# The projection's seventh product by quarter products, with GpSimd adding its parts

## Chip, cores and metric

The kernel runs on one core of one Trainium2 chip. The metric is the device time of one execution in microseconds (us). The kernel before takes 3261.11 us, the median of 3 runs (3260.39 to 3261.24).

TensorE is called PE in the profile and here, its weight loads PEld, VectorE DVE, ScalarE ACT, GpSimd POOL, and SP is the engine that issues the transfers.

## The reference

The reference applies two layers of the same form to x of shape (8, 512, 32, 32), all in fp32. One layer, cut to what matters (the layers differ in the number of groups and in their weights):

```python
xn = group_norm(x) * gn_scale + gn_bias            # (B, 512, N), N = 32 * 32
q, k, v = split(einsum('oc,bcn->bon', qkv_w, xn) + qkv_b)   # 8 heads of 64
attn = softmax(einsum('bhdi,bhdj->bhij', q, k) / sqrt(64))
out = einsum('bhij,bhdj->bhdi', attn, v)
return einsum('oc,bcn->bon', proj_w, out) + proj_b + x
```

The last line is the projection with which this change deals: a 512x512 weight matrix times a 512x1024 matrix for each of 8 batches in 2 layers.

## The kernel before, in words

The kernel goes through 16 units, one for each layer and batch. Each unit u does its three input projections (`projections`: q, k, v), then the output projection of the unit before it (`project(old, after)`), then its own attention (`attention`). The projection of unit 15 stands at the end and has a function of its own (`project_last`). So `project` runs 15 times, in units 1 to 15.

**Seven products in place of eight.** `blocks` computes a matrix product in a Strassen-Winograd form. Both matrices are cut into 2x2 blocks, sums and differences of blocks are made beforehand (`left[k]` and `right[k]`, k from 1 to 7), and seven products of blocks, 256x256 by 256x512, are added up. In `blocks` they come in the order 1, 6, 2, 7, 5, 4, 3, with the banks of PSUM called bx (`apair[0]`), by (`sbank[0]`) and bz (`apair[1]`): 1 and 2 write bx, 6, 7 and 4 write by, 5 and 3 write bz. Product 7 accumulates onto product 6 in by. Engines DVE and ACT take intermediate results out: p1 is product 1, u2 is p1 plus product 6, u3 is p1 plus products 6 and 7. Then the blocks of the result are c11, and by `others` u3 + product 5 for (1, 1), p1 + product 4 on by for (1, 0), and u2 + product 5 + product 3 for (0, 1).

**Quarter products.** A product k named in `INNER` is cut once more in the same way: seven matmuls of 128x256 in place of four matmuls of 128x512 (`inner_products`, with the matmul on line L458; an uncut product runs in `block_product`, L419). Its seven steps write as follows. Steps 2, 3 and 4 accumulate into the product's own bank. Steps 1, 6 and 7 accumulate one after the other onto a quarter of a helper bank `one`, and ACT copies the running sum out after each of them (L463). Step 5 writes a helper bank `two` and is copied too. So a step 6 or 7 can start only when ACT has copied what stood in `one` before it. The four copies land in a room in SBUF (`rest`, in the profile m_o for the projection). `fold` (L471, L472) has GpSimd add them up in place, and `rests` (L748) has GpSimd add the room into the finished result, after which it is stored. The order of the steps is one of three tuples:

```python
ORDER, ORDER_5, ORDER_1 = (1, 2, 3, 6, 5, 4, 7), (1, 5, 2, 6, 3, 4, 7), (2, 3, 1, 4, 5, 6, 7)
```

ORDER_1 is used for product 1 of k. There, and for no other product, the last step is not run in its place: `inner_products` returns it, and the next uncut product runs it between its own matmuls.

**The projection.** `project` calls `blocks` with products 2, 3 and 4 cut (tiles ro, their right factors, and lo, their left factors); product 7 is uncut. After each product `done` runs: DVE adds bias and residual to u2, u3 and p1 (`plus`, L706), and DVE takes the statistics of the next unit's input (L283). `others` takes banks on DVE (L740). Attention's first scores wait for the takes of (1, 0), the third scores for those of (0, 1).

**Right and left factors.** The right factors of the projection come from the attention output ao. The list `parts` in `attention` puts the subtractions on DVE (`mix_right` L179, `mix_inner_in` L209 to L212, `mix_o` L1019) behind numbered steps of the next unit's `projections`: steps 15 to 21 lie in v. The left factors of the cut products are the same for all units of a layer. GpSimd makes them once per layer (`mix_inner_left`, L226 to L232, four additions for each product), and they are stored in memory and loaded in each unit (tiles lo and a spare quarter of ro). Layer 0's are made in unit 0, layer 1's for the projection in unit 9. In unit 7, GpSimd also makes three sets of left factors of layer 1's q (tile lw), inside `project`, after its third `done`.

**Order of work.** The schedule is manual: each engine runs its instructions in the order in which the code issues them. The framework adds the semaphores that data and buffers need.

Of the kernel before, what the change touches and what calls it, by code (L numbers as in the profile page):

```python
# [11 lines left out]
F32 = mybir.dt.float32  # L12
# [20 lines left out]
def fast_path(ctx, tc, x, qkv_wT, proj_wT, vecs, groups, out, flag):  # L33
# [24 lines left out]
    BL = 32  # L58
    SCALE = 1.0 / math.sqrt(D)

    INNER = {"q": (2, 5, 4, 3), "k": (1, 2, 7, 5, 4, 3), "o": (2, 3, 4)}
    assert D == H and C == FD

    def pool(name, bufs, **kw):
# [358 lines left out]
                )  # L423

    def blocks(name, left, right, tokens, c11, others, done, u3_in, summed, inner={}, rests=None,
               u2_in=(trpool, "tr"), between=None, behind=None, p1=None):

        bx, by, bz = apair[0], sbank[0], apair[1]
        sums, taken = [], []

        def products(bank, k, start, stop, between=None):
            block_product(bank, left[k], right[k], tokens, start, stop, between)

        def inner_products(bank, k, first=False):  # L440

            if k not in inner:
                products(bank, k, first, k != 5)
                return None
            a, b, one, two, order, room = inner[k]
            one, two, rest = one[:, 0, :FD2], two[:, 0, :FD2], room(f"m{k}_{name}")
            dst = {
                1: one, 6: one, 7: one, 5: two,  # L450
                2: bank[:, 0, :FD2], 3: bank[:, 0, FD2:], 4: bank[:, 1, :FD2],
            }
            to = {
                1: rest[:, 0, :FD2], 6: rest[:, 0, FD2:], 7: rest[:, 1, :FD2], 5: rest[:, 1, FD2:]
            }

            def step(j):
                nc.tensor.matmul(  # L458
                    dst[j], a[j], b[j], start=j in (1, 5) or first and j in (2, 4),
                    stop=j not in (1, 6), skip_group_check=True,  # L460
                )
                if j in to:
                    taken.append(nc.scalar.copy(to[j], dst[j]))  # L463

            for j in order if k != 1 else order[:-1]:
                step(j)
            return (rest, partial(step, order[-1])) if k == 1 else rest

        def fold(rest):
            add = nc.gpsimd.tensor_add  # L470
            add(rest[:, 0, FD2:], rest[:, 0, FD2:], rest[:, 1, FD2:])  # L471
            add(rest[:, 1, FD2:], rest[:, 1, :FD2], rest[:, 1, FD2:])  # L472

        def add_rest(r, h, rest, alone=None):

            if rest is not None:
                fold(rest)
                rests(r, h, rest, alone)

        def work(pool, tag, k):  # L480
            sums.append(pool.tile([P, 2, FD], F32, tag=tag, name=f"{k}_{name}"))
            return sums[-1]

        fresh = p1 is not None or 1 in inner
        if p1 is not None:
            sums.append(p1)
            done(sums)
            products(by, 6, True, False)
        elif fresh:
            p1 = work(accpool, "acc", "p1")  # L490
            rest, last = inner_products(bx, 1, True)
            done(sums)
            products(by, 6, True, False, last)
            add = nc.vector.tensor_add
            add(rest[:, 0, FD2:], rest[:, 0, FD2:], rest[:, 1, FD2:])
            add(p1[:, 0, :], bx[:, 0, :], rest[:, 0, :])
            add(p1[:, 1, :FD2], bx[:, 1, :FD2], rest[:, 1, :FD2])
            add(p1[:, 1, FD2:], rest[:, 1, :FD2], rest[:, 1, FD2:])
        else:
            products(bx, 1, True, False, between)  # L500
            if behind is not None:
                behind()
            p1 = work(accpool, "acc", "p1")
            nc.scalar.copy(p1, bx)  # L504
            done(sums)
            products(by, 6, True, False)
        u2 = work(*u2_in, "u2")
        summed(0, u2, by, p1)
        done(sums)
        rest = inner_products(bx, 2, fresh)  # L510
        c11(bx, p1 if fresh else None, rest)
        add_rest(0, 0, rest)
        done(sums)
        seventh = inner_products(by, 7)
        u3 = work(*u3_in, "u3")
        summed(1, u3, by, p1)
        if seventh is not None:
            fold(seventh)
        done(sums)
        twice = inner_products(bz, 5, True)  # L520
        others(1, 1, bz, u3, twice)
        add_rest(1, 1, twice, u3)
        if seventh is not None:
            rests(1, 1, seventh)
        done(sums)
        rest = inner_products(by, 4)
        others(1, 0, by, p1)
        add_rest(1, 0, rest)
        if seventh is not None:
            rests(1, 0, seventh)  # L530
        done(sums)
        rest = inner_products(bz, 3)
        others(0, 1, bz, u2, twice)
        add_rest(0, 1, rest, u2 if twice is not None else None)
        if twice is not None:
            rests(0, 1, twice)
        done(sums)
        return taken[-1:]
# [159 lines left out]
    def project(w, after):  # L698


        l, b = units[w.u]
        dst = mid[b] if l == 0 else out[b]
        g = 0

        def plus(to, o, cols, more):
            return nc.vector.scalar_tensor_tensor(  # L706
                to, cols, vec[:, l, PB, o : o + 1], more, ALU.add, ALU.add
            )

        def done(sums):  # L710

            nonlocal g
            g += 1
            for i in range(2):
                if g == 2:
                    u2 = sums[1][:, i, :]
                    plus(u2, i, w.res[i][:, FD:], u2)
                elif g == 4:
                    u3 = sums[2][:, i, :]
                    plus(u3, 2 + i, w.res[2 + i][:, FD:], u3)  # L720
                elif g == 5:
                    p1 = sums[0][:, i, :]
                    plus(p1, 2 + i, w.res[2 + i][:, :FD], p1)
            after(g)

        results = {}

        def store(o, h):
            nc.sync.dma_start(dst[o * P : (o + 1) * P, ts(h, FD)], results[o, h])

        def c11(bank, *_):
            for i in range(2):
                cols = results[i, 0] = w.res[i][:, :FD]
                plus(cols, i, bank[:, i, :], cols)

        def others(r, h, bank, more, _=None):
            for i in range(2):
                o = 2 * r + i
                results[o, h] = more[:, i, :]
                w.evac[h] = nc.vector.tensor_add(more[:, i, :], bank[:, i, :], more[:, i, :])  # L740
                if (r, h) == (1, 1):
                    store(o, h)

        def rests(r, h, rest, _):
            for i in range(2):
                o = 2 * r + i
                cols = results[o, h]
                nc.gpsimd.tensor_add(cols, cols, rest[:, i, :])  # L748
                store(o, h)

        w.evac = [None, None]
        x, z, s1 = apair[0], apair[1], sbank[1]
        tmp = room_of(tmppool, "tmp")
        plan = {
            2: (s1, z, ORDER, tmp), 4: (x, s1, ORDER, tmp), 3: (s1, x, ORDER, room_of(accpool, "acc"))
        }
        inner = {k: (*w.inner_o[k], *plan[k]) for k in w.inner_o}
        w.taken = blocks(
            f"o_{w.u}", w.left, w.right_o, False, c11, others, done, (rbpool, "rb"), plain_sum, inner, rests
        )  # L760

    def project_last(w, rest):
# [25 lines left out]
    def attention(w, at_step, at_end):  # L788
# [188 lines left out]
        def bias_last():  # L977
# [4 lines left out]

        parts = {
            3: [lambda: reciprocals(CC - 1)], 10: [lambda: divide(CC - 1)], 14: [bias_last],
            17: mixing[:2], 21: [mixing[3], mixing[2]],
        }

        w.inner_o = {}
# [15 lines left out]
            w.making[i](lefts[3 * i : 3 * i + 3], later=behind_loads)  # L1004

        def mix_o(k):
            tag = {2: "x2", 3: "x1", 4: "x4"}[k]
            room = tpool.tile([P, 4, FD2], F32, tag=tag, name=f"ro{k}_{u}")
            if k == INNER["o"][-1]:
                w.inner_o[k] = mix_inner_in(w.right_o[k], room, nc.vector)  # L1010
                lefts.append(room[:, 3, :P])
                if u == B:
                    make_left(2)
                else:
                    nc.sync.dma_start(lefts[-1], src[:, len(lefts) - 1, :])
            else:
                w.inner_o[k], subs = mix_inner(w.right_o[k], room, nc.vector)
                for part in subs:
# [4 lines left out]
                w.inner_o[k] = (inner_lefts(k, w.left[k], lefts[3 * i : 3 * i + 3]), w.inner_o[k])  # L1023

        parts[15] = [load_left]
        if u == B:
            parts[20] = [partial(make_left, 0), partial(make_left, 1)]
        parts[18] = [partial(mix_o, 2)]
        parts[21] += [partial(mix_o, 4), partial(mix_o, 3)]
        w.finish = finish  # L1030
        return parts

# [451 lines left out]
```

## Time and profile before

| | us | share of the span |
|---|---|---|
| span of the profiled run | 3260.1 | |
| PE busy | 3247.2 | 100% |
| DVE busy | 2713.7 | 83% |
| ACT busy | 1650.7 | 51% |
| POOL busy | 1238.9 | 38% |

A row of the profile names the line of the kernel, the engine, the operation, what it writes and reads, and shapes. A row of a timeline begins with the start and the duration in us, merges equal instructions (x8 is eight of them), and ends in brackets with the idle time of the engine just before and what released it. Each matmul of the code is two records on PE[...]. The ends of matmuls are modelled, and overlap the next start; distances from start to start are what counts. A row of the waits reads: engine and line that waited, who released it, total us, times, longest us.

### The profile page before, as it was taken

What the parts mean: (1) busy time and instruction counts of PE and PEld (TensorE: products, weight loads), DVE (VectorE), ACT (ScalarE), POOL (GpSimd) and SP (SyncE); (2) the same over time, 40 slices, a digit from 0 to 9 for tenths busy, and PEclk for the clock granted to TensorE, in tenths of its full rate; (3) what the DMA queues carried; (4) which work ended last, traced back from release to release, by engine and by line L of the source; (5) the groups of instructions that cost most, each with busy time, mean ns of one, the idle gap of its engine ahead of it and who ended that gap; (6) DMA issues with size and microseconds to landing.
All of it is one profiled execution on the core that took longest, in us unless ns stands there. A gap on an engine that the chain in (4) does not pass through costs nothing.

```text
span 3260.1 us, 56861 instructions
## 1 busy us (share of the span) xinstructions
PE 3247.2 (100%) x22206; PEld 1858.1 (57%) x22206; DVE 2713.7 (83%) x3460; ACT 1650.7 (51%) x2296; POOL 1238.9 (38%) x1235
## 2 busy tenths in 40 slices
PE   9999999999999999999999999999999999999999
PEld 5456474654746547465474655747556474564743
DVE  5887978889788897889978889797897978979777
ACT  1653726536274463744637446374563735637354
POOL 2054071531706317065470632607226071350710
PEclk9999999999999999999999999999999999999999
DMA  3112120121201212023120121201212012120221
GB/s 102 43 52 79 44 78 28 49 79 46 79 28 45 79 46 87 20 71 107 58 89 29 45 80 52 85 15 45 86 46 85 15 49 82 46 85 15 70 74 48
DMA packets 86465, 192.53 MB, mean 59 GB/s; under 512 B 22960, under 2 KB 34992, under 8 KB 84272
## 3 DMA queue, kind: packets, MB, share of 16 engines
q1 hardware_dynamic: 86192, 188.82, 17.0%
q8 instruction: 180, 2.95, 0.4%
q14 instruction: 93, 0.76, 0.1%
HBM read 148.00 MB, written 39.19 MB: 57 GB/s over the span
## 4 chain that ended last, share of the span: by engine, by line
PE 97%; DVE 1%; issue 1%; ACT 0%; DMA 0%; SPq 0%; DVEq 0%; ACTq 0%
PE a L851 26%; PE s L823 25%; PE s L419 14%; PE a L419 12%; PE a L458 10%; PE s L458 9%; PE a L823 1%; DVE acc L870 1%; PE s L769 0%; PE a L769 0%; PE s L364 0%; DVE tr L883 0%; DMA xn<-x_dram 0%; DVE acc L868 0%; ACT p L831 0%
## 5 line engine op out<-in xcount | busy, mean ns | idle before, releaser
L831 ACT ACTIVATE p<-s 128x1024 f32<-128x1024 f32 x976 | 997.0, 1023 | 560.4 <-PE s L823 526.3
L851 PE MATMUL a<-p,v 64*64 64x512 f32 x8192 | 1098.2, 589 | 1.7 <-ACT p L831 1.5
L823 PE MATMUL s<-q,k 64*64 64x512 f32 x7808 | 1056.4, 590 | 0.0
L870 DVE TENSOR_TENSOR acc<-acc,p 128x1024 f32<-128x1024 f32 x768 | 964.0, 1255 | 71.1 <-ACT p L831 18.1
L851 PEld LDWEIGHTS a<-p,v 64*64 64x64 f32 x8192 | 381.0, 131 | 500.5 <-ACT p L831 352.8
L823 PEld LDWEIGHTS s<-q,k 64*64 64x64 f32 x7808 | 380.1, 133 | 435.3 <-issue 425.6
L1080 POOL TENSOR_TENSOR r<-xn 128x256 f32<-128x256 f32 x30 | 51.2, 1707 | 1126.3 <-DVE acc L870 1049.0
L653 POOL TENSOR_TENSOR k<-k,m_k 128x512 f32<-128x512 f32 x180 | 259.7, 1464 | 0.0
L868 DVE TENSOR_TENSOR acc<-p,p 128x1024 f32<-128x1024 f32 x128 | 157.6, 1231 | 23.0 <-ACT p L831 13.9
L883 DVE STREAM_TRANSPOSE tr<-acc 128x1024 f32<-128x1024 f32 x128 | 157.9, 1233 | 0.0
L315 POOL TENSOR_TENSOR y<-var,half 128x4 f32<-128x4 f32 (+1 forms) x17 | 33.1, 1949 | 327.2 <-DVE var L313 327.2
L653 POOL TENSOR_TENSOR q<-q,m_q 128x512 f32<-128x512 f32 x120 | 157.1, 1325 | 0.0
L893 DVE TENSOR_REDUCE red<-tr 128x32 f32<-128x1024 f32 x128 | 153.9, 1202 | 0.5
L541 DVE TENSOR_TENSOR u_v<-s,p_v 128x1024 f32<-128x1024 f32 x32 | 39.2, 1224 | 124.6 <-PE s L419 122.3
L877 DVE TENSOR_TENSOR ao<-a,tmp 128x512 f32<-128x512 f32 x128 | 87.9, 687 | 65.9 <-ACT tmp L876 65.9
L504 ACT COPY p_o<-a 128x1024 f32<-128x1024 f32 x15 | 15.2, 1012 | 244.2 <-PE a L419 244.2
L471 POOL TENSOR_TENSOR m_o<-m_o 128x256 f32<-128x256 f32 x45 | 34.0, 756 | 253.9 <-ACT m_o L463 253.9
L463 ACT COPY m_q<-s 128x256 f32<-128x256 f32 x150 | 55.8, 372 | 145.8 <-PE s L458 143.1
L419 PE MATMUL s<-x_t,s2w 128*128 128x512 f32 x256 | 117.5, 592 | 0.0
L419 PE MATMUL a<-w,xn 128*128 128x256 f32 x496 | 112.1, 379 | 0.0
L463 ACT COPY m_k<-s 128x256 f32<-128x256 f32 x165 | 61.4, 372 | 93.9 <-PE s L458 90.3
L337 ACT ACTIVATE xn<-xn,shift,scale 128x512 f32<-128x512 f32 x124 | 99.5, 804 | 12.4 <-DVE shift L333 12.2
(283 smaller groups left out, 5150.5 us busy)
## 6 DMA issues: line engine op xcount, KB each, us to landing
rb<-drec SPq DMA_DIRECT2D x128, 256.0 KB, 3.8
xn<-mid SPq DMA_DIRECT2D x36, 512.0 KB, 7.6
il<-ilk SPq DMA_DIRECT2D x15, 1152.0 KB, 6.6
xn<-x_dram SPq DMA_DIRECT2D x32, 512.0 KB, 7.2
x<-x_dram SPq DMA_DIRECT2D x32, 512.0 KB, 5.3
x<-mid SPq DMA_DIRECT2D x28, 512.0 KB, 4.8
il<-ilq SPq DMA_DIRECT2D x15, 768.0 KB, 4.2
mid<-u_o SPq DMA_DIRECT2D x32, 256.0 KB, 2.1
```

The source lines that it names most:

```text
L337: nc.scalar.activation(cols, cols, AF.Identity, bias=st["shift"][:, c - lo : c - lo + 1], scale=st["scale"][:, c - lo : c - lo + 1],)
L419: nc.tensor.matmul(dst, at[:, c, ts(i, P)], moving[:, c, :], start=start and c == 0 and not (tokens and i % 2), stop=stop and c == 1, skip ...
L458: nc.tensor.matmul(dst[j], a[j], b[j], start=j in (1, 5) or first and j in (2, 4), stop=j not in (1, 6), skip_group_check=True,)
L463: taken.append(nc.scalar.copy(to[j], dst[j]))
L653: w.last[sel].append(add(cols, cols, rest[:, i, :]))
L823: nc.tensor.matmul(bank[e * H : (e + 1) * H, j, :], w.k[pr][j * H : (j + 1) * H, t * P + e * H : t * P + (e + 1) * H], w.q[pr][j * H : (j ...
L831: exp = nc.scalar.activation(p, bank, AF.Exp, scale=SCALE)
L851: nc.tensor.matmul(banks[r][j * H : (j + 1) * H, :], w.v[rows, t, lo : lo + D], p[rows, j, :], start=(t == 0), stop=(t == NT - 1),)
L868: nc.vector.tensor_add(acc, state["first"], p)
L870: nc.vector.tensor_add(acc, acc, p)
L883: nc.vector.transpose(tr, state["acc"].pop(c))
L893: nc.vector.tensor_reduce(red[:, :, qh, :], state["tr"].rearrange("p j (f i) -> p j f i", i=BL), AX.X, ALU.add)
```

## The change

Product 7 of the projection is cut into quarter products too, so that its four matmuls of 512 columns become seven of 256. It uses the helper banks `one` = sbank[1] and `two` = apair[1], ORDER_1 as order of the steps, and the room o2.

Its parts have to be added into two results, (1, 1) and (1, 0). For (1, 0) GpSimd adds the folded room into p1 itself (`into_p1`), before DVE adds the bias to p1 and before the takes; for (1, 1) `rests` adds it after the take, and `rests` now also stores (1, 1). Product 3's room moves from the pool accpool to o1, as the right factors of product 7 get a tile from accpool. The subtraction `mixing[3]` moves one step ahead (20 in place of 21), because product 7's right factor comes from it.

```diff
-    INNER = {"q": (2, 5, 4, 3), "k": (1, 2, 7, 5, 4, 3), "o": (2, 3, 4)}
+    INNER = {"q": (2, 5, 4, 3), "k": (1, 2, 7, 5, 4, 3), "o": (2, 3, 7, 4)}
...
         if seventh is not None:
             fold(seventh)
+            if into_p1:
+                for i in range(2):
+                    nc.gpsimd.tensor_add(p1[:, i, :], p1[:, i, :], seventh[:, i, :])
         done(sums)
...
-        if seventh is not None:
+        if seventh is not None and not into_p1:
             rests(1, 0, seventh)
...
-                if (r, h) == (1, 1):
-                    store(o, h)
-
-        def rests(r, h, rest, _):
+
+        def rests(r, h, rest, _=None):
...
         plan = {
-            2: (s1, z, ORDER, tmp), 4: (x, s1, ORDER, tmp), 3: (s1, x, ORDER, room_of(accpool, "acc"))
+            2: (s1, z, ORDER, tmp), 7: (s1, z, ORDER_1, room_of(tpool, "o2")),
+            4: (x, s1, ORDER, tmp), 3: (s1, x, ORDER, room_of(tpool, "o1")),
         }
...
-            17: mixing[:2], 21: [mixing[3], mixing[2]],
+            17: mixing[:2], 20: [mixing[3]], 21: [mixing[2]],
...
-            tag = {2: "x2", 3: "x1", 4: "x4"}[k]
-            room = tpool.tile([P, 4, FD2], F32, tag=tag, name=f"ro{k}_{u}")
-            if k == INNER["o"][-1]:
+            pool, tag = {2: (tpool, "x2"), 7: (accpool, "acc"), 3: (tpool, "x1"), 4: (tpool, "x4")}[k]
+            room = pool.tile([P, 4, FD2], F32, tag=tag, name=f"ro{k}_{u}")
+            if k in (7, 4):
                 w.inner_o[k] = mix_inner_in(w.right_o[k], room, nc.vector)
-                lefts.append(room[:, 3, :P])
-                if u == B:
-                    make_left(2)
-                else:
-                    nc.sync.dma_start(lefts[-1], src[:, len(lefts) - 1, :])
+                n = len(lefts)
+                lefts.extend(room[:, 3, i * P : (i + 1) * P] for i in range(2))
+                if u != B:
+                    nc.sync.dma_start(
+                        room[:, 3, :].rearrange("p (s o) -> p s o", s=2), src[:, n : n + 2, :]
+                    )
...
         parts[15] = [load_left]
+        parts[18] = [partial(mix_o, 2)]
+        parts[20].append(partial(mix_o, 7))
+        parts[21] += [partial(mix_o, 4), partial(mix_o, 3)]
         if u == B:
-            parts[20] = [partial(make_left, 0), partial(make_left, 1)]
-        parts[18] = [partial(mix_o, 2)]
-        parts[21] += [partial(mix_o, 4), partial(mix_o, 3)]
+            parts[20] += [partial(make_left, i) for i in range(3)]
+            parts[21].append(partial(make_left, 3))
```

More of the change, by code (lines that the diff above doesn't have):

```diff
@@ L425, in blocks @@
     def blocks(name, left, right, tokens, c11, others, done, u3_in, summed, inner={}, rests=None,
-               u2_in=(trpool, "tr"), between=None, behind=None, p1=None):
+               u2_in=(trpool, "tr"), between=None, behind=None, p1=None, into_p1=False):
         bx, by, bz = apair[0], sbank[0], apair[1]
@@ L758, in project @@
         w.taken = blocks(
-            f"o_{w.u}", w.left, w.right_o, False, c11, others, done, (rbpool, "rb"), plain_sum, inner, rests
+            f"o_{w.u}", w.left, w.right_o, False, c11, others, done, (rbpool, "rb"), plain_sum, inner, rests,
+            into_p1=True,
         )
```

## The prediction

> **What bounds the kernel now.** I read the page's busy shares and chain first, to see which engine sets the end.
>
> ```profile
> PE 3247.2 (100%) x22206; PEld 1858.1 (57%) x22206; DVE 2713.7 (83%) x3460; ACT 1650.7 (51%) x2296; POOL 1238.9 (38%) x1235
> PE 97%; DVE 1%; issue 1%; ACT 0%; DMA 0%; SPq 0%; DVEq 0%; ACTq 0%
> ```
>
> TensorE (PE) is busy for 3247 of 3260 us and is 97% of the chain. So a matmul saved is time saved, and a gap opened on PE is time lost. The list of PE's waits says how few gaps there are (total us, times, longest):
>
> ```profile
> PE s L364 <- DMA xn<-x_dram: 4.3, 1, 4.3
> PE a L851 <- ACT p L831: 1.5, 1, 1.5
> PE s L419 <- DVE xn L179: 0.3, 1, 0.3
> ```
>
> There is no slack on PE in which a new wait could hide. Next the timeline of PE in the second projection (start, us, operation; x2 is one product of 256 columns[...]):
>
> ```profile
> 476.81 0.59 PE L458 MATMUL s<-ao,wproj_wproj 128*128 128x256 f32 x2
> ...
> 479.40 0.59 PE L458 MATMUL s<-ro,wproj_wproj 128*128 128x256 f32 x2
> 479.83 3.60 PE L419 MATMUL s<-ao,wproj_wproj 128*128 128x512 f32 x8
> 483.27 3.60 PE L419 MATMUL a<-o_t,s1w 128*128 128x512 f32 x8
> ```
>
> From start to start: product 2, already done by seven quarter products, takes 479.83 - 476.81 = 3.02 us (0.43 a step); product 7, done by four matmuls of 512 columns, takes 483.27 - 479.83 = 3.44 us.
>
> ScalarE (ACT) takes the partial sums of a quarter product out of PSUM. Its timeline beside that product:
>
> ```profile
> 477.44 0.37 ACT L463 COPY m_o<-s 128x256 f32<-128x256 f32 x1 [2.81 <-PE s L458]
> ...
> 480.03 0.37 ACT L463 COPY m_o<-s 128x256 f32<-128x256 f32 x1 [0.49 <-PE s L458]
> ```
>
> The copies start 0.63 us after their step starts (477.44 - 476.81, 480.03 - 479.40) and last 0.37: a sum is taken 1.00 us after its step began. In ORDER, (1,2,3,6,5,4,7), two other steps stand between steps 1, 6 and 7, which share one bank; a step is due 3 x 0.43 = 1.29 us after the one before it there, so PE never waits.
>
> How long PE needs to start after a release is seen in its one stall in a projection, at 1825 us:
>
> ```profile
> 1823.93 1.22 DVE L179 TENSOR_TENSOR xn<-xn 128x1024 f32<-128x1024 f32 x1
> 1824.26 0.59 PE L458 MATMUL s<-r,w 128*128 128x256 f32 x2
> 1825.20 0.30 PEld L419 LDWEIGHTS s<-xn,w 128*128 128x128 f32 x2 [0.75 <-DVE xn L179]
> 1825.20 3.70 PE L419 MATMUL s<-xn,w 128*128 128x512 f32 x8 [0.35 <-DVE xn L179]
> 1825.74 0.19 PEld L419 LDWEIGHTS s<-xn,w 128*128 128x128 f32 x1 [0.24 <-issue]
> ```
>
> The operand is ready at 1825.15. The weight load starts at 1825.20. The later load at 1825.74 runs, as everywhere in the stream, 0.43 after the first matmul, which so began at 1825.31: 0.16 us after the release.
>
> [...] Here ACT starts 0.04 us after the recorded end, so I use the 0.63 from the step's start, not the estimate. [...] PE pulls weight loads ahead of running matmuls. It does, by 0.21 us (load at 477.03 for the matmul at 477.24), but in the stall above the load waited too. [...] the same L706 pair on DVE takes 1.42 us with GpSimd idle and 1.82 beside its additions.
>
> **The change part by part.** There are 15 projections of this form (units 0 to 14, done within units 1 to 15); the last has its own function.
>
> *Removed*: four 512-column matmuls for seven of 256, 3.44 - 3.02 = 0.42 us of PE, 15 times: -6.3 us.
>
> *The order of the new steps.* Product 7 uses ORDER_1, (2,3,1,4,5,6,7). Steps 1, 6 and 7 write sbank[1], and ACT must take the sum after 1 and after 6. From 1 to 6 there are two steps between: no wait. From 6 to 7 there is none. In the key projection that uses ORDER_1 today the last step is held back into the next product, which hides this; for product 7 the code runs the whole order at once. In the built program step 7 does wait for ACT. Step 6 starts at t, its copy ends at t + 1.00, step 7 starts at t + 1.16 in place of t + 0.43: 0.73 us of idle PE. Lower bound 0.57 (no release time); upper 0.90 (0.12 to the load, 0.21 from load to matmul as in the running stream). Behind step 7 stand product 5 and all else of PE. 15 x 0.73 = +11.0 us (8.6 to 13.5).
>
> Step 1 follows product 2's step 7 in the same bank with two steps between, so it is free.
>
> *Additions with one answer.* Four copies more on ACT (1.5 us), which is idle for 7.0 us at that place. Four subtractions of 128x256 on DVE (0.42 each) and the 1.22 us subtraction that moves forward: 2.9 us into the 2.23 us that DVE idles before 470.14; the take of the value product slips some 0.7 us, nobody waits for its bank until 478.5, and DVE is 1.2 us lighter afterwards. The extra weights' 128 KB land in 1.8 us, over 8 us ahead of use. The fourth set-up of left factors in unit 0 and unit 9 is four GpSimd additions of 0.46 us, before a GpSimd wait of 1.56 us and before product 2's folding. I cost all these at nothing.
>
> *The new wait of DVE on GpSimd.* DVE's bias addition to p1 (L706) must now wait until GpSimd has folded product 7 (2 x 0.73) and added two 128x512 parts (2 x 1.27): 4.0 us. Queued behind it on DVE are the takes of products 4 and 3, and attention's first scores wait for these. In an ordinary unit GpSimd is free at 483.7, has p1 ready at about 487.8 [...], and DVE needs the first half at 488.5 and the second at 489.2. It fits; the chain to the scores has over 2 us beyond that. But in unit 7 GpSimd makes the next layer's left factors just there:
>
> ```profile
> 1491.82 0.46 POOL L226 TENSOR_TENSOR lw<-w 128x128 f32<-128x128 f32 x1
> ...
> 1498.42 0.45 POOL L232 TENSOR_TENSOR lw<-w,lw 128x128 f32<-128x128 f32 x1
> 1498.83 0.73 POOL L471 TENSOR_TENSOR m_o<-m_o 128x256 f32<-128x256 f32 x1
> 1499.64 0.73 POOL L472 TENSOR_TENSOR m_o<-m_o 128x256 f32<-128x256 f32 x1
> 1500.33 2.51 POOL L748 TENSOR_TENSOR p_o<-p_o,m_o 128x512 f32<-128x512 f32 x2
> ```
>
> ```profile
> 1496.35 1.79 DVE L706 SCALAR_TENSOR_TENSOR p_o<-x,vec,p_o 128x512 f32<-128x512 f32 x2
> 1498.06 1.28 DVE L740 TENSOR_TENSOR p_o<-s,p_o 128x512 f32<-128x512 f32 x2
> ```
>
> The four rows from 1498.83 on are just the new work's shape: p1 would be whole at 1502.8, the L706 pair ends at 1503.6 (first half starts at 1501.6), and the L740 pair at 1504.9. Attention's first scores, which start at 1500.9 (1501.2 with the step above), need that pair: they start at 1505.1, 3.9 late. The third scores need the last takes, behind two statistics: 1504.9 + 1.28 + 1.29 = 1507.5 against 1506.8, 0.8 more. Sum +4.7 us, once. Lower bound 3 (faster additions), upper 6.5 ([...] as the u_o additions of 3.49 in place of 2.50 us show).
>
> *Sum*: -6.3 + 11.0 + 4.7 = +9.4 us: 3261.1 + 9.4 = 3270.5 us. All low: -6.3 + 8.6 + 3 = +5.3, 3266.4. All high: -6.3 + 13.5 + 6.5 = +13.7, 3274.8.
>
> **Rivals.**
> (a) *PE's new stall is real but unit 7's is absorbed*: 3261.1 - 6.3 + 11.0 = 3265.8. For it: DVE has idle pieces there (0.54 us before its last take). Against: they sum to far less than 5 us.
> (b) *No stall between steps 6 and 7* (the copy is quicker or the wait points elsewhere): not slower, 3261.1 - 6.3 = 3254.8, or 3259.5 with unit 7's. For it: PE shows hardly a wait with this code today. Against: the copies between steps start 0.63 us after their step, and all of them last 0.36 to 0.37 us.
> (c) *DVE waits for GpSimd in every unit*: GpSimd gets 6.5 us more per projection (2 x 0.73 + 4 x 1.27), [...] each unit's first scores are late by about 1 us: 3270.5 + 15 = 3285. Against: the slack counted above.
>
> **How the numbers follow.** Forecast 0.65; (a) 0.10; (b) 0.12; (c) 0.13. The range 3265 to 3276 holds the forecast's bounds and (a), and the light end of (c). The 0.2% bounds are 3254.6 and 3267.6. Slower: nine tenths of the forecast and (c), 0.71. Within: the rest of the forecast, (a), and most of (b), 0.25. Faster: 0.04.
>
> **What would show it.** In the profile of after: product 7's steps 2 to 6 at a pitch of 0.43 us and then a step 7 about 1.16 after step 6; PE's list of waits with a new row on ACT m_o, 15 times, about 0.57 each (0.73 less the 0.16 by which the recorded end outlasts the pitch); product 7 from start to start near 3.75 us. In unit 7 alone a wait of DVE L706 on GpSimd of about 5 us, and one of the scores of about 4 us. I am wrong if step 7 comes 0.43 after step 6, if L706 waits on GpSimd in ordinary units, or if PE waits anywhere else in the projections.

## The result, and the profile after

The changed kernel takes 3287.56 us (median of 4 runs, 3286.17 to 3288.21) against 3261.18 us of the kernel before (3260.39 to 3261.63): ratio 1.0081, 95% interval 1.0063 to 1.0098. It is slower by 26 us, where 9.4 were forecast.

The page of after, its line of busy times and its line of the chain by engine:

```profile
PE 3249.8 (99%) x22296; PEld 1949.5 (59%) x22296; DVE 2794.4 (85%) x3520; ACT 1675.4 (51%) x2356; POOL 1380.6 (42%) x1333
PE 92%; DVE 5%; issue 2%; POOL 1%; ACT 0%; DMA 0%; DVEq 0%; POOLq 0%; ACTq 0%
```

PE's share of the chain fell from 97% to 92%, and DVE's rose from 1% to 5%. So DVE has come onto the path in some places. PE's waits in after name the places (total us, times, longest):

```profile
PE s L459 <- ACT m_o L464: 6.9, 15, 0.5
PE s L827 <- DVE p_o L744: 5.7, 1, 5.7
PE s L827 <- POOL m_o L473: 4.9, 14, 1.5
...
PE a L827 <- DVE u_o L744: 2.7, 12, 0.3
```

All four are new. The first is the wait between steps 6 and 7, in each of the 15 projections. The second is unit 7. The third and fourth are attention's first and third scores (L827), late in nearly every unit. The releaser named in the third row misleads: the first scores write the bank (s) out of which DVE's L744 takes product 4, and the fold (L473) works on the room alone. They start 0.36 us after that last take ends in unit 1 (289.11 + 1.28 = 290.39, then 290.75) and in unit 7 alike (1511.05 + 1.27 = 1512.32, then 1512.68), where the fold's L473 starts only after them.

TensorE's timeline in unit 1 of after (start, us, idle before in brackets):

```profile
279.27 0.59 PE L459 MATMUL s<-ro,lo 128*128 128x256 f32 x2
280.33 0.70 PE L459 MATMUL s<-ao,wproj_wproj 128*128 128x256 f32 x2 [0.46 <-ACT m_o L464]
280.87 3.60 PE L419 MATMUL a<-o_t,s1w 128*128 128x512 f32 x8
...
290.75 1.95 PE L827 MATMUL s<-q,k 64*64 64x512 f32 x16 [0.25 <-POOL m_o L473]
```

Product 5 (280.87) begins one step's pitch of 0.43 after step 7, which so began at 280.44: 1.17 after step 6. The first scores then wait. DVE in the same stretch, and GpSimd beside it:

```profile
284.55 1.29 DVE L744 TENSOR_TENSOR u_o<-a,u_o 128x512 f32<-128x512 f32 x2 [0.57 <-issue]
285.76 3.43 DVE L710 SCALAR_TENSOR_TENSOR p_o<-x,vec,p_o 128x512 f32<-128x512 f32 x2
289.11 1.28 DVE L744 TENSOR_TENSOR p_o<-s,p_o 128x512 f32<-128x512 f32 x2
```

```profile
282.79 2.94 POOL L522 TENSOR_TENSOR p_o<-p_o,m_o 128x512 f32<-128x512 f32 x2
285.69 2.95 POOL L750 TENSOR_TENSOR u_o<-u_o,m_o 128x512 f32<-128x512 f32 x2
```

The same bias pair for p1 in an ordinary unit (unit 2) of before, the takes behind it, and the first scores:

```profile
488.16 1.41 DVE L706 SCALAR_TENSOR_TENSOR p_o<-x,vec,p_o 128x512 f32<-128x512 f32 x2
489.49 1.29 DVE L740 TENSOR_TENSOR p_o<-s,p_o 128x512 f32<-128x512 f32 x2
```

```profile
492.84 1.95 PE L823 MATMUL s<-q,k 64*64 64x512 f32 x16
```

This is the heart of the result. GpSimd has all of p1 ready at 285.73 (282.79 + 2.94). DVE is busy with the takes of (1, 1) until then (284.55 + 1.29 = 285.84), and its pair follows without idle time, so DVE does not wait for p1. In 14 of the 15 units the trace shows no idle time there. But the pair lasts 3.43 us in place of 1.41, just while GpSimd adds the parts to u3 for (1, 1) (L750, itself 2.95). The takes of (1, 0) end 2.0 us later for it, and the first scores follow them.

Distances between fixed points of PE's timeline put a size on each place. "To the scores" is from product 1's first matmul to the first scores; "to the third" is from the first scores to the third; "unit" is from one product 1 to the next:

```
               to the scores   to the third     unit
ordinary unit  22.89 -> 23.53   1.77 -> 2.17   201.6 -> 202.7
unit 7         22.89 -> 29.26   1.77 -> 3.17   203.5 -> 211.9
unit 8         22.89 -> 23.63   1.77 -> 2.07   202.2 -> 202.8
unit 9         22.89 -> 25.45   1.77 -> 2.27   201.6 -> 204.7
```

In unit 7 the forecast wait is there. DVE's pair, the first scores, and GpSimd's next additions:

```profile
1507.72 3.40 DVE L710 SCALAR_TENSOR_TENSOR p_o<-x,vec,p_o 128x512 f32<-128x512 f32 x2 [4.41 <-POOL p_o L522]
1511.05 1.27 DVE L744 TENSOR_TENSOR p_o<-s,p_o 128x512 f32<-128x512 f32 x2
```

```profile
1512.68 3.35 PE L827 MATMUL s<-q,k 64*64 64x512 f32 x16 [5.72 <-DVE p_o L744]
```

```profile
1508.86 3.39 POOL L750 TENSOR_TENSOR u_o<-u_o,m_o 128x512 f32<-128x512 f32 x2
```

Here, too, the pair takes 3.40 us beside L750. And the first 16 scores take 3.35 us in place of 1.95. The table of windows around them says why (us from start; busy PE, PEld, DVE, ACT, POOL, each with its instructions; PEclk, DMA share, GB/s):

```profile
1512.00:1514.00 2.00, 1.32 (x8) 0.61 (x12) 2.00 (x4) 0.00 (x0) 1.92 (x4) 0.54 0.42 154
1514.00:1516.00 2.00, 2.00 (x16) 0.70 (x12) 1.89 (x4) 1.02 (x1) 2.00 (x2) 0.61 0.12 42
```

The granted clock was half (0.50) for 3.4 us, from 1512.15 to 1515.57, after PE had stood still for 5.7 us.

### The profile page after: what moved, and what is told of

Read it like the earlier page. It is cut to its first block, busy times and chain, and to the rows that moved or that the text cites. A ratio compares the mean times of both kernels' runs of the same rounds, so it can differ in the third digit from the quotient of the medians.

```text
span 3284.0 us, 57352 instructions
## 1 busy us (share of the span) xinstructions
PE 3249.8 (99%) x22296; PEld 1949.5 (59%) x22296; DVE 2794.4 (85%) x3520; ACT 1675.4 (51%) x2356; POOL 1380.6 (42%) x1333
## 4 chain that ended last, share of the span: by engine, by line
PE 92%; DVE 5%; issue 2%; POOL 1%; ACT 0%; DMA 0%; DVEq 0%; POOLq 0%; ACTq 0%
PE a L855 26%; PE s L827 24%; PE s L419 12%; PE a L419 11%; PE a L459 8%; PE s L459 8%; PE a L827 1%; DVE u_o L744 1%; DVE p_o L710 1%; DVE acc L874 1%; DVE p_o L744 0%; DVE stats L283 0%; PE s L773 0%; PE a L773 0%; PE s L364 0%
## 5 line engine op out<-in xcount | busy, mean ns | idle before, releaser
L855 PE MATMUL a<-p,v 64*64 64x512 f32 x8192 | 1122.5, 589 | 2.2 <-ACT p L835 2.0
L827 PE MATMUL s<-q,k 64*64 64x512 f32 x7808 | 1081.0, 591 | 10.6 <-DVE p_o L744 5.7
L874 DVE TENSOR_TENSOR acc<-acc,p 128x1024 f32<-128x1024 f32 x768 | 979.3, 1275 | 68.7 <-ACT p L835 14.5
L855 PEld LDWEIGHTS a<-p,v 64*64 64x64 f32 x8192 | 409.5, 131 | 472.6 <-ACT p L835 330.7
L827 PEld LDWEIGHTS s<-q,k 64*64 64x64 f32 x7808 | 427.7, 133 | 401.0 <-issue 382.1
L472 POOL TENSOR_TENSOR m_o<-m_o 128x256 f32<-128x256 f32 x60 | 50.9, 849 | 169.0 <-ACT m_o L464 168.9
L464 ACT COPY m_o<-s 128x256 f32<-128x256 f32 x150 | 55.9, 372 | 113.2 <-PE s L459 110.5
L750 POOL TENSOR_TENSOR u_o<-u_o,m_o 128x512 f32<-128x512 f32 x60 | 111.8, 1883 | 0.1
```

Of the source, the lines that this page charges most:

```text
L827: nc.tensor.matmul(bank[e * H : (e + 1) * H, j, :], w.k[pr][j * H : (j + 1) * H, t * P + e * H : t * P + (e + 1) * H], w.q[pr][j * H : (j ...
L855: nc.tensor.matmul(banks[r][j * H : (j + 1) * H, :], w.v[rows, t, lo : lo + D], p[rows, j, :], start=(t == 0), stop=(t == NT - 1),)
L874: nc.vector.tensor_add(acc, acc, p)
```

## The experiments

The theory after the traces ("overlap"): DVE's p1 pair, which has two inputs in SBUF (the on-chip memory), and GpSimd's additions hold each other up when they run beside each other (3.43 us in place of 1.41, and 2.95 in place of 2.50, in unit 1 of after). This makes the takes late in every unit. The rival ("data"): DVE is late because it now waits for p1 from GpSimd. Beside these stand two separate losses, the step wait and unit 7. Lines differ by a few between kernels; times are changes against after (3287.6 us) unless said.

**a_order**: product 7 in the other order, and the halves of product 5 and of (1, 1) turned round.

```diff
-            2: (s1, z, ORDER, tmp), 7: (s1, z, ORDER_1, room_of(tpool, "o2")),
+            2: (s1, z, ORDER, tmp), 7: (z, s1, ORDER, room_of(tpool, "o2")),
...
+            halves = (1, 0) if into_p1 and k == 5 else (0, 1)
+            block_product(bank, left[k], right[k], tokens, start, stop, between, halves)
...
-            for i in range(2):
+            for i in (1, 0) if (r, h) == (1, 1) else (0, 1):
```

> The changed kernel, but product 7 runs with the helper banks exchanged (one = apair[1], two = sbank[1]) in ORDER, so that two steps stand between steps 1, 6 and 7; product 5, which writes apair[1] next, does its second half first. If the wait between steps 6 and 7 costs 0.74 us each time and its end sets everything behind it: -11.0 us, 3276.5. If VectorE is late for a reason of its own, at the end of the projection, part of it comes back as a longer wait of the first scores: from the rows of the changed kernel I reckon with 0.57 of the 0.74, 3279. If that lateness hangs on GpSimd alone, nearly all of it comes back: 3286.

It took 3276.74 us, ratio to before 1.0048 (1.0031 to 1.0065): -10.8. The size fits and the reason does not. The step wait is not gone, it has moved to product 5 (PE's waits, then DVE and GpSimd in unit 2, of this kernel):

```profile
PE a L419 <- ACT m_o L465: 6.9, 15, 0.5
```

```profile
488.05 2.42 DVE L711 SCALAR_TENSOR_TENSOR p_o<-x,vec,p_o 128x512 f32<-128x512 f32 x2
```

```profile
488.21 3.39 POOL L751 TENSOR_TENSOR u_o<-u_o,m_o 128x512 f32<-128x512 f32 x2 [0.20 <-DVE u_o L745]
```

Product 5's first matmul waits for the copy of product 7's last sum, although it now writes the other half of that two-bank tile: turning the halves round does not lift the wait. What gained the time is the turned order of halves. The pair begins where it did in after (18.53 us after product 1), but GpSimd's additions for (1, 1) now start after it, the pair takes 2.42 us, and the scores no longer wait (23.21 to the scores, 1.77 to the third).

**b_later**: GpSimd's additions for (1, 1) moved behind product 4's work; nothing else.

```diff
-        if seventh is not None:
+        if seventh is not None and not into_p1:
             rests(1, 1, seventh)
...
-        if seventh is not None and not into_p1:
-            rests(1, 0, seventh)
+        if seventh is not None:
+            rests(1, int(into_p1), seventh)
```

> The changed kernel, but GpSimd adds product 7's parts into (1, 1) after product 4's work in place of before it. [...] (GpSimd's additions into u3 and VectorE's bias additions to p1, each with two SBUF inputs, [...] 3.43 us a pair in place of 1.41, and the takes and scores behind are late): pair back to 1.4 to 2.0 us, the scores' waits of 0.32 and 0.40 us gone in all units, unit 7 about 2 better: 3287.6 - 15 x 0.7 - 2 = 3275. Data theory (VectorE waits for GpSimd to finish p1): no change, 3287.

3276.38 us, ratio 1.0048 (1.0031 to 1.0065): -11.2. DVE's pair in unit 2 is back to its time of before:

```profile
486.83 1.41 DVE L710 SCALAR_TENSOR_TENSOR p_o<-x,vec,p_o 128x512 f32<-128x512 f32 x2
```

To the scores 23.21 and to the third 1.77 in ordinary units, though DVE still needs p1 from GpSimd and the step wait (6.9, 15 times) is as it was. This is close to the overlap theory's number; the data theory falls. The 2 us expected from unit 7 did not come: it lasts 212.2 us, as the clock stood at 0.50 for 6.8 us there (1504.75 to 1511.58), and the first 16 scores took 3.69 us in place of 1.95. The run also gives the step wait's size apart from the rest: 23.21 against the 22.48 below, 0.73 us.

**c_lw**: in unit 7, the next layer's left factors made after the last `done` of the projection in place of the third.

```diff
-                    for part, room in zip(made_parts[:3], rooms) if g == 3 else ():
+                    for part, room in zip(made_parts[:3], rooms) if g == 7 else ():
```

> The changed kernel, but the left factors that GpSimd makes within the projection of unit 7 come after its last product in place of after its third. If they are what made this unit's scores 5.7 us late (with half a clock for 3.4 us behind it), the unit comes back to the length of the others, about -7.4 us: 3280. If the unit was late for the half clock alone: -1.5, 3286.

3280.25 us, ratio 1.006 (1.0043 to 1.0077): -7.3 where 7.4 were expected. That the number fits is in part chance. Unit 7's wait of the scores shrinks to 1.6 us, and the clock stays at 1.00, but the unit is only 4.6 us shorter (207.3 in place of 211.9) and not back at an ordinary length. Another 0.7 us lie in unit 12, where GpSimd happened to have p1 0.25 us later, so that its additions met only the second half of DVE's pair: the pair took 2.45 us, and no scores waited.

**d_all**: the three edits together.

> The three edits together. If the step wait, the additions beside p1's and unit 7's left factors are all that the change lost, only the saved steps are left: 3261.2 - 6.3 = 3255, faster than before. If VectorE still waits for GpSimd's p1: 3265 or more.

3269.48 us, ratio 1.0025 (1.0015 to 1.0035): 14 us more than expected. The step wait, which a_order was to cure, is still there, 15 times (0.73 each, 11.0 in all), and unit 7 (206.2 us) and unit 9 (203.5) remain 2.7 and 2.0 longer than in before. The pair is back to its time of before, 1.41 us in unit 2 (489.85).

**g_hold**: step 7 held back and run between the halves of product 5, as product 1 of k does it today; the fold and the additions to p1 stand behind it.

```diff
+    ORDER_7 = (2, 3, 1, 5, 4, 6, 7)
...
-            for j in order if k != 1 else order[:-1]:
+            held = k == 1 or into_p1 and k == 7
+            for j in order[:-1] if held else order:
                 step(j)
-            return (rest, partial(step, order[-1])) if k == 1 else rest
+            return (rest, partial(step, order[-1])) if held else rest
...
-        twice = inner_products(bz, 5, True)
+        twice = inner_products(bz, 5, True, last)
```

> The changed kernel, but product 7's steps run as 2, 3, 1, 5, 4, 6, and step 7 is held back and run between the two halves of product 5; GpSimd folds and adds behind it. TensorE's wait before step 7 should be gone: 0.74 us a projection, if nothing takes its place -11, 3277. But GpSimd gets product 7's last part about 1 us later beside an earlier product 5, and in the changed kernel VectorE's lateness then ends at the scores: if their wait grows by the same, 3287; I expect part of it, 3280.

3273.32 us, ratio 1.0038 (1.0023 to 1.0054): -14.2, more than expected. The step wait is gone from PE's list, and to the scores it is 22.51, 1.02 less than in after. DVE's pair in unit 2 is still long (3.16 us), but starts earlier (17.81 us after product 1 in place of 18.53). So DVE is just in time for the first scores, and nearly all of their 0.32 us of wait goes with the step wait. But to the third it still is 2.17, and unit 7 still waits 6.4 us.

**i_old**: after with the old way of adding, that is, product 7's parts added to the results of (1, 1) and (1, 0) after the takes (`into_p1=True` left out), so that DVE waits for GpSimd nowhere.

> The changed kernel without the additions into p1: GpSimd adds product 7's parts into (1, 1) and (1, 0) after the takes, as the key projection does. If what made the scores late is that p1's bias additions stand beside GpSimd's additions of any sort [...], they still stand beside those into (1, 1), which now come right with them: waits of the scores stay at about half or more, 3281 to 3287. If it is the wait for p1's data, they are gone, in unit 7 too: 3287.6 - 11 - 7 = 3270.

3279.47 us, ratio 1.0057 (1.0042 to 1.0073): -8.1, a little under the overlap theory's 3281 to 3287, and far from the data theory's 3270. Without any wait of DVE on p1, its pair is long again beside GpSimd (unit 2, DVE and GpSimd):

```profile
487.82 3.06 DVE L710 SCALAR_TENSOR_TENSOR p_o<-x,vec,p_o 128x512 f32<-128x512 f32 x2
```

```profile
487.38 2.94 POOL L750 TENSOR_TENSOR u_o<-u_o,m_o 128x512 f32<-128x512 f32 x2 [2.50 <-DVE u_o L744]
```

The pair is 0.37 us shorter than in after, and the first scores are just on time then (23.21). The third are not (2.11), and attention gets new waits on DVE, 12 of them, 3.0 us in all. So an ordinary unit lasts as long as in after (202.6 to 202.7 us): freeing DVE of p1 gained nothing there. Most of the 8.1 us lie in unit 7, which lasts 206.4 us in place of 211.9.

**e_add and f_memset**: the disputed cost by itself, on the kernel before. At the place where DVE's p1 pair starts, GpSimd gets work that nobody reads: two additions, or six memsets (three for each i), into an unused half of a tile (x in the rows below). The edit with the additions; the other has six `memset` in their place, held back by a dependency on the same take:

```diff
+            if (r, h) == (1, 1):
+                for i in range(2):
+                    spare = w.res[2 + i][:, FD:]
+                    nc.gpsimd.tensor_add(spare, more[:, i, :], more[:, i, :])
```

> The kernel before, with two extra GpSimd additions of 128x512 that read u3 from SBUF (their result goes to an unused tile and is read by nobody), released by the take of (1,1), so that they run beside DVE's p1 pair L706, and nothing else of the change. In before that pair takes 1.41 us with GpSimd idle. [...] the pair takes 2.4 to 3.4 us and the additions 2.9 to 3.4 in place of 2.5; the takes of (1,0) come 1.0 to 2.0 us later. In before the first scores have about 2.1 us of slack, so the time stays within 0.2 us per projection of before, or loses up to 0.3 us per projection at the top end: 3261 to 3266. Data theory (the pair is long in after because of what it waits for): the pair stays at 1.41 us and the time at 3261.

> The counterpart of the one with two additions: at the same place GpSimd runs six memsets of 128x512 to the same unused tile, which read nothing from SBUF but keep GpSimd about as long busy. If the lengthening comes from GpSimd reading SBUF [...], the p1 pair stays at 1.41 us, or lengthens by less than 0.3 us; if any GpSimd access to SBUF has the same effect, it takes 2.4 us or more as with the additions. Time 3261 (slack hides either).

e_add, DVE and GpSimd in unit 2:

```profile
486.48 2.60 DVE L706 SCALAR_TENSOR_TENSOR p_o<-x,vec,p_o 128x512 f32<-128x512 f32 x2
```

```profile
486.05 2.48 POOL L746 TENSOR_TENSOR x<-u_o 128x512 f32<-128x512 f32 x2 [4.00 <-DVE u_o L740]
```

f_memset, the same:

```profile
486.23 1.41 DVE L706 SCALAR_TENSOR_TENSOR p_o<-x,vec,p_o 128x512 f32<-128x512 f32 x2
```

```profile
486.38 3.32 POOL L747 MEMSET x<- 128x512 f32 x6 [4.58 <-DVE u_o L740]
```

Additions beside it make the pair 2.60 us long; memsets, though GpSimd is busy for longer, leave it at 1.41. So GpSimd's being busy does not hold DVE up by itself. The additions read SBUF and the memsets do not; that this reading is the cause fits both runs, but it is not shown apart from their other differences. In e_add the additions themselves were not stretched, against the expectation, and the pair gained 1.2 us, not the 2.0 of after. e_add takes 3263.60 us, ratio 1.0007 (0.9998 to 1.0015), no difference that can be told, and the way to the scores is 22.89 as before: in that kernel the slack holds a pair 1.2 us longer. f_memset takes 3267.12 us, ratio 1.0017 (1.0009 to 1.0025), 5.8 us more than before. This was not expected: its ways to the scores and to the third are those of before. In its profiled run, which took 3264.44 us, the largest loss is in unit 7 behind the third scores (206.3 us in place of 203.5). Why is open.

**h_best**: g_hold, b_later and c_lw together.

> The last edit together with the late additions into (1, 1) and the late left factors of unit 7. Nothing of the three losses should be left but rests of unit 7 (1.4 us) and unit 9 (1.5 us): 3261.4 - 6.3 + 3 = 3258, 0.1% faster than before. If the additions into p1 make VectorE late even so: 3262 to 3269.

3260.26 us, ratio 0.9997 (0.9989 to 1.0005): no difference from before that can be told. In ordinary units everything the change was to save is there: 22.48 to the scores, 0.41 us less than before, and 1.77 to the third. PE in unit 2 with the held step between the halves of product 5:

```profile
481.75 1.88 PE L419 MATMUL a<-o_t,s1w 128*128 128x512 f32 x4
483.46 0.59 PE L459 MATMUL s<-ao,wproj_wproj 128*128 128x256 f32 x2
```

The two bad units give it back, more than the 3 us that were expected: unit 7 lasts 206.2 us against 203.5 of before, unit 9 203.6 against 201.6.

**j_best**: h_best, with two subtractions of the next layer's weights on DVE in unit 7 moved behind the last take.

```diff
-            for g, lo, hi in ((15, 0, 4), (17, 4, 6), (20, 6, 8)):
+            for g, lo, hi in ((15, 0, 4), (17, 4, 6)):
...
+                    if g == 7:
+                        mix_coming(6, 8)
```

> The kernel that holds step 7 back and has GpSimd add the parts of u3 later and make the next layer's left factors later (3260.3), with the last two DVE subtractions of the next layer's weights (0.68 us each) in unit 7 moved from behind the end of v to behind the last take of the projection. In the kernel it starts from, unit 7's PE waits are 0.66 (a step of product 4 on DVE), 0.4 (first scores), 0.2 and 0.2 (third scores, and a step of attention), as DVE is about 1.4 us late there. If DVE's lateness comes from these subtractions, the first two go and unit 7 loses 1.5 to 1.9 us: 3258.6. If it comes from the four quarter subtractions of product 7's right factor, they stay: 3260.3. Either way the sum leaves unit 9 (+3 us against before) as it is.

3260.53 us, ratio 0.9998 (0.9989 to 1.0006). Half right: unit 7 now reaches the scores in 22.48 us (24.18 in h_best), so these subtractions were what made DVE late there. But the unit as a whole lasts 206.0 us, hardly less than 206.2: attention loses what the projection gained. Neither version beats the kernel before.

## Why the prediction was wrong, by its own steps

The direction was right, the time was 17 us too low and outside the range. Each term, with what it measured (a unit's share of the first two, -0.41 + 0.73 = 0.32, is taken out of the others):

| term | forecast | measured |
|---|---|---|
| seven steps for four matmuls | -0.42 x 15 = -6.3 | 22.48 - 22.89 = -0.41, x 15 = -6.2 |
| step 7 waits for the copy | +0.73 x 15 = +11.0 | 23.21 - 22.48 = 0.73, x 15 = +11.0 |
| unit 7 | +4.7 | 211.9 - 203.5 - 0.3 = +8.1 |
| ordinary units, takes late | 0 | (0.32 + 0.40) x 13 = +9.4 |
| unit 9 | 0 | 204.7 - 201.6 - 0.3 = +2.8 |
| sum | +9.4 | +25.1 |

The two profiled spans differ by 23.9 us (3284.0 - 3260.1). The fourth term is an upper figure: in unit 15 the wait for the third scores is missing, in unit 8 it is 0.1 shorter.

*Right.* The saving, the step wait and its place: step 7 came 1.17 after step 6 (1.16 forecast), PE's new row shows 15 waits, 6.9 us in all (0.46 each, 0.57 forecast), and product 7 takes 280.87 - 277.11 = 3.76 us (3.75). L710 waits for GpSimd in unit 7 (4.41 us, about 5 forecast), and in ordinary units not at all, as forecast.

*Wrong: "It fits; the chain to the scores has over 2 us beyond that".* This is the step that failed. It asked when p1 would be ready, and that was answered nearly right (about 487.8 forecast; 469.82 + 18.51 = 488.33 in unit 2 of after). It did not ask what GpSimd does next, and so put nothing on DVE's own pair. When DVE's pair starts, GpSimd goes on to the additions for (1, 1), which the same change gave it, and the pair takes 3.43 us in place of 1.41. With the step wait's delay the takes end 23.17 after product 1 began, 2.33 later than in before (490.78 - 469.94 = 20.84). PE reaches its scores only 0.32 later. The "over 2 us" were less than they looked: of the 2.06 from the last take to the first scores in before (492.84 - 490.78) the release takes 0.36, so 1.70 were free. 2.33 - 0.32 - 1.70 leaves the wait of about 0.32 us at the first scores. The third scores stand behind the same queue and lose 0.40 more. b_later moved just these additions and had both back; i_old took away the wait on p1 and still had the long pair; e_add made the pair long with nothing else.

The row for it was in the prediction, "1.42 us with GpSimd idle and 1.82 beside its additions". But those additions, in unit 7 of before, are the small ones of 128x128 that make left factors (the prediction's rows of lw). It was read as the size of the effect, where it was the size beside additions of 128x128. The traces show how it grows with the addition that stands beside one of the two instructions of the pair:

| GpSimd addition beside it | the addition alone, us | one DVE instruction, us | gained |
|---|---|---|---|
| none | | 0.74 | |
| 128x128 (before, unit 7) | 0.46 | 0.93 | 0.19 |
| 128x256 (h_best, unit 7) | 0.73 | 1.21 | 0.47 |
| 128x512 (after) | 1.25 | 1.75 | 1.01 |

So in these runs a DVE instruction gained up to the addition's own time less about 0.25 us; in e_add the two of the pair gained 0.41 and 0.78.

The runs show on what the length hangs: the pair takes 2.60 us beside additions and 1.41 beside memsets, and in the table its gain grows with the addition's length. DVE's takes, which read one input from a bank of PSUM, stay at 0.67 to 0.69 us each in all units of after (L744, 90 of them), beside additions too (unit 1, 284.55). How the engines come to hold each other up is not shown. They do not simply run one after the other: in e_add pair and additions lie within 3.03 us (486.05 to 489.08), where one after the other they would fill 1.41 + 2.48 = 3.89.

*Wrong in size: unit 7.* The mechanism was forecast. The first scores come 29.26 after product 1, where the forecast's rows give 1505.1 - 1478.0 = 27.1. Of the 2.2 us, 0.7 is p1 being whole later (25.5 after product 1, forecast 24.8), and 1.4 the pair at 3.40 us, against 2.0 in the forecast: the same cause again, as GpSimd's additions for (1, 1) lie beside it. The 1.4 more to the third scores, where 0.8 was forecast, is the half clock: 16 scores in 3.35 us in place of 1.95. The half clock lasted 3.4 us after the gap of 5.7, and there was none in c_lw, whose gap was 1.6. In a_order, b_later and g_hold, with gaps of 5.2 to 6.4 us, it lasted 6.8 us. The forecast put no price on a slower clock; whether a gap of 3.9 us, as forecast, would have brought one is not shown.

*Wrong: unit 9 at nothing.* GpSimd's fourth set of left factors was costed as idle time of GpSimd. It runs beside DVE's subtractions, which take 0.56 to 0.67 us in place of 0.42 there, and DVE comes late to product 6 (unit 9 of after, PE):

```profile
1908.56 0.70 PE L459 MATMUL s<-ao,wproj_wproj 128*128 128x256 f32 x2 [0.36 <-DVE u_o L545]
```

The first scores then wait 1.5 us. This is read from the trace; no run took the set away by itself. The four subtractions and the moved one, costed at nothing too, are free in ordinary units, but not in unit 7, where DVE also makes the next layer's weights. There DVE starts on u3's bias pair 16.34 us after product 1 in place of 14.10. In after the wait for GpSimd hides this; h_best shows it, and j_best takes it away. The loads of left factors, now 128 KB each, landed in 2.1 us (1.8 forecast, the time of the 64 KB loads of before).

Rival (c) was nearest in time (3285), with about 1 us lost per unit, but not by its own mechanism. It looked for the loss in a late p1, for which DVE would wait in every unit; that wait is in unit 7 alone, and the loss was in the pair after it. Rival (b) falls by the 15 waits, and (a) by unit 7's 5.7 us.

## What to carry to other kernels

When work is moved to GpSimd, ask not only whether its result is ready in time, but which DVE instructions with two SBUF inputs stand beside each of the added instructions, and price each of those at its own time plus nearly the addition's (0.74 us became up to 1.75 beside additions of 1.25 us here, where takes with one input in PSUM stayed at 0.67 to 0.69). Moving the additions that nobody waits for past DVE's critical instructions gave back 11 us here. An accumulating product whose last step waits for a copy is worth its fewer matmuls only if other work is put in front of that step: here the wait took 0.73 us where the matmuls saved 0.41, and held back behind half a product the step cost nothing (22.48 to the scores in h_best, 22.89 in before).

## What the runs showed of the hardware

- Beside GpSimd additions of 128x512, a DVE pair of scalar_tensor_tensor on 128x512 in fp32 took 2.42 to 3.43 us in place of 1.41; the additions' pair took 2.48 to 3.40 in place of 2.50. One instruction of the DVE pair took 0.74 us alone, 0.93 beside additions of 128x128, 1.21 beside 128x256 and up to 1.75 beside 128x512. Beside memsets of GpSimd the pair stayed at 1.41. DVE's takes, with one input in PSUM, took 0.67 to 0.69 us each in all units of after, beside additions too.
- After a gap of 5.7 us on PE (after, unit 7) the granted clock was 0.50 for 3.4 us, after gaps of 5.2 to 6.4 us (a_order, b_later, g_hold) for 6.8 us. The drop came 3.0 to 5.2 us after the recorded end of the last matmul (b_later: 1501.77, then 1504.75; after: 1506.96, then 1512.15). In c_lw, whose longest wait there was 1.6 us, the clock stayed at 1.00.
- Six memsets per projection on GpSimd, beside which neither DVE's pair nor the way to the scores was longer, made the whole 5.8 us slower; the cause is open.
